# An attention layer's score products on four row strips of the array, and the next chunk's maxima moved into the present chunk's loop

## The chip, the cores and the metric

The kernel runs on one core of one Trainium2 chip. The metric is the device time of one execution in microseconds (us). Executions of one kernel agree within about 0.1% here. "Clock" is the TensorE clock that the profile records as granted, 1.00 being full speed. In the views, PE is TensorE, PEld the loading of its weights, DVE VectorE, ACT ScalarE and POOL GpSimd; L443 is line 443 of that kernel. PSUM is the memory to which the products are written; "a bank" stands below for the room of one tile of 512 columns in it.

## The reference

Four layers follow one another on x of shape (4, 64, 64, 128): a selective-scan block, an attention over all 4096 positions of an image, a convolution block and a neighborhood attention. Only layer 1, the attention, is touched. As the two kernels compute it, for each of the four images:

```
f = x @ Wq            # (4096, 16)
g = x @ Wk            # (4096, 16)
h = x @ Wv            # (4096, 128)
scores[n, m] = f[n] . g[m]
p = softmax over n of scores           # its maximum over n is subtracted first
x = x + gamma * (sum over n of h[n] * p[n, m])
```

The inner dimension of a score is 16. With one further row for the maximum to be subtracted it is 17, on an array of 128 rows.

## The kernel before

f and g lie transposed (channels on partitions). Row 32 of f is 1 and row 32 of g is minus the maximum, so that a product gives the shifted score. All other rows are zero, and every product spans all 128 rows. A first phase computes all scores only to take their maxima. A second computes them again, takes exp, and multiplies with the values; the scores of the next key tiles can be issued while exp runs, because four score tiles are in use.

```python
# phase 1: maxima
for j in range(NJ):                                    # 32 tiles of 128 queries
    for half in range(2):
        ps = psum.tile([128, 4, 512], F32, name="ps_max")          # two buffers
        for q in range(4):
            n0 = half * 2048 + q * 512
            nc.tensor.matmul(ps[:, q, :], gT[:, j * 128 : (j + 1) * 128], fT[:, n0 : n0 + 512], ...)
        nc.vector.tensor_reduce(mx[:, j, half : half + 1], ps, AX.XY, ALU.max)
# ... cut: minus the maxima go to row 32 of gT ...
# phase 2: exp and values
for c in range(NCH):                                   # 8 chunks of 512 queries
    # ... cut ...
    for j in range(NJ):                                # 32 tiles of 128 keys
        ps = psum.tile([128, 512], F32, name="ps_s", bufs=4)
        nc.tensor.matmul(ps, fT[:, j * 128 : (j + 1) * 128], gT[:, cols], start=True, stop=True)
        e = pool.tile([128, 512], F32, name="e", bufs=4)
        nc.scalar.activation(e, ps, AF.Exp)
        nc.tensor.matmul(pa, hv[:, j, :], e, start=(j == 0), stop=(j == NJ - 1))
        # ... cut: esum += e on VectorE ...
    # ... cut: denominator (ones x esum), reciprocal, product, x += gamma * ...
```

Of the kernel before, what the change touches and what calls it, by code (L numbers as in the profile page):

```python
"""Four layers on x (4, 64, 64, 128): a VMamba block (four-direction selective scan and an
MLP), an attention over all positions, a CSP conv block, a neighborhood-attention block.

Layouts, for one image of 4096 tokens and 128 channels:
- "rows":  [128, 32, 128], partition p and slot j hold token p * 32 + j  (layers 0 and 1)
- "tiles": [128, 32, 128], partition p and slot j hold token j * 128 + p (layer 3)
- transposed: channels on partitions, tokens along the free axis.
Layer 1 reshapes its (C, N) result to (N, C): row c, column j * 128 + p of it is token
c * 32 + j, channel p, which is the "rows" layout of its residual.
"""  # L10
# [28 lines left out]
# Neighborhood attention, by pairs of query rows: (first slot of the row's window among the  # L39
# eight key rows, first row of the position bias) for the upper and the lower query row.  # L40
# [3 lines left out]
def bc(ap, shape):  # L44
    return ap.to_broadcast(list(shape))


def mid(ap, n):
    """[p, f] -> [p, n, f], every n the same."""
    return bc(ap.unsqueeze(1), [ap.shape[0], n, ap.shape[1]])  # L50


# ---------------------------------------------------------------------------------------
# shared parts
# ---------------------------------------------------------------------------------------
# [19 lines left out]
def layernorm_T(tc, K, pool, psum, x, w, b, put):  # L75
    """LayerNorm over the channels of x [128, 32, 128]; put(g) is where the transposed,
    scaled and shifted slots 4g..4g+3 go, as [128 channels, 4, 128]."""
# [22 lines left out]
def mlp_residual(tc, K, pool, psum, x, xnT, w1, b1, w2, b2row):  # L100
    """x += gelu(xn @ w1 + b1) @ w2 + b2 for the 32 slots of x, xnT in the slots' order."""
# [19 lines left out]
def transpose_rows(tc, K, psum, x, xT):  # L121
    """x in "rows" -> xT [128 channels, 4096 tokens in order]."""
    nc = tc.nc
    view = xT.rearrange("c (p j) -> c j p", j=NJ)
    for g in range(NJ // 4):
        pt = psum.tile([128, 4, 128], F32, name="ps")
        for t in range(4):
            nc.tensor.transpose(pt[:, t, :], x[:, 4 * g + t, :], K.ident)
        if g % 2:
            nc.scalar.copy(view[:, 4 * g : 4 * g + 4, :], pt)  # L130
        else:
            nc.vector.tensor_copy(view[:, 4 * g : 4 * g + 4, :], pt)


# ---------------------------------------------------------------------------------------
# layer 0
# ---------------------------------------------------------------------------------------
# [38 lines left out]
def conv3x3(nc, out, lhsT, src, row0, nrows):  # L176
    """Accumulate the nine taps of a SAME 3x3 convolution into out [128, nrows, 64];
    src is [128, 64, 64], lhsT(tap) the weights. Taps off the image are left out."""
# [13 lines left out]
def layer0(tc, K, P, x):  # L192
    """x in "rows", updated in place."""
# [80 lines left out]
def selective_scan(tc, K, P, xc, yacc):  # L274
    """yacc = the four directions' scans of xc [128, 2, 4096], each with its skip term, on
    the tokens' own places. A direction runs over chunks of 512 tokens; the state after a
    chunk is the next one's initial value."""
    nc = tc.nc
    with ExitStack() as ctx:
# [3 lines left out]
        # The 40 rows (dt, B, C) of a chunk; the rest stays 0.  # L283
# [4 lines left out]
        def places(t, k, c):  # L288
            """Chunk c of direction k in t [128, 4096]: rows of the image, or columns."""
# [7 lines left out]
        def prepare(k, c, xdbl):  # L297
# [17 lines left out]
            # softplus(s) = max(s, 0) + log1p(e), e = exp(-|s|);  # L315
            # log1p(e) = ln(u) - ((u - 1) - e) with u = 1 + e as rounded.
# [57 lines left out]
# ---------------------------------------------------------------------------------------  # L374
# layer 1
# ---------------------------------------------------------------------------------------
def load_layer1(ctx, tc, K, A):
    nc = tc.nc
    pool = ctx.enter_context(tc.tile_pool(name="w1", bufs=1))
    P = SimpleNamespace()  # L380
    for name, shape in (("Wq", [128, 16]), ("Wk", [128, 16]), ("Wv", [128, C]), ("gamma", [128, 1])):
        t = pool.tile(shape, F32, name=f"w1_{name}")
        src = A[f"L1_conv_{name}"]
        nc.sync.dma_start(t, src.partition_broadcast(128) if name == "gamma" else src)
        setattr(P, name, t)
    return P


def layer1(tc, K, P, x):
    """x in "rows", updated in place. scores[n, m] = f[n] . g[m], softmax over n. Row 32 of  # L390
    f and g holds 1 and -max over n, so a product of the two is the shifted score. The other rows are 0,
    so that a product spans all 128 rows of the array."""
    nc = tc.nc
    with ExitStack() as ctx:
# [5 lines left out]
        mx = big.tile([128, NJ, 2], F32, name="mx")  # L400
        nmx = big.tile([128, NJ], F32, name="nmx")
        nc.gpsimd.memset(fT, 0.0)
        nc.gpsimd.memset(gT, 0.0)
        nc.gpsimd.memset(fT[32:33, :], 1.0)
        with tc.tile_pool(name="l1_ap", bufs=8, space=PSUM) as psum:
            transpose_rows(tc, K, psum, x, xT)
            for c in range(NCH):
                cols = slice(c * 512, (c + 1) * 512)
                for t, w in ((fT, P.Wq), (gT, P.Wk)):
                    ps = psum.tile([128, 512], F32, name="ps")  # L410
                    nc.tensor.matmul(ps[:16, :], w, xT[:, cols], start=True, stop=True)
                    nc.vector.tensor_copy(t[0:16, cols], ps[:16, :])  # L412
# [5 lines left out]
        with tc.tile_pool(name="l1_bp", bufs=2, space=PSUM) as psum:  # L418
            for j in range(NJ):
                for half in range(2):  # L420
                    ps = psum.tile([128, 4, 512], F32, name="ps_max")
                    for q in range(4):
                        n0 = half * 2048 + q * 512
                        nc.tensor.matmul(  # L424
                            ps[:, q, :], gT[:, j * 128 : (j + 1) * 128], fT[:, n0 : n0 + 512],
                            start=True, stop=True,
                        )
                    nc.vector.tensor_reduce(mx[:, j, half : half + 1], ps, AX.XY, ALU.max)  # L428
        nc.vector.tensor_reduce(nmx, mx, AX.X, ALU.max, negate=True)
        with tc.tile_pool(name="l1_c", bufs=3) as pool, tc.tile_pool(name="l1_cp", bufs=2, space=PSUM) as psum:  # L430
            for c in range(NCH):
                pr = psum.tile([1, 512], F32, name="pr", bufs=1)
                for t in range(4):
                    j = 4 * c + t
                    nc.tensor.transpose(pr[:, t * 128 : (t + 1) * 128], nmx[:, j : j + 1], K.ident)
                nc.vector.tensor_copy(gT[32:33, c * 512 : (c + 1) * 512], pr)
            for c in range(NCH):
                cols = slice(c * 512, (c + 1) * 512)
                pa = psum.tile([128, 512], F32, name="pa")
                esum = pool.tile([128, 512], F32, name="esum", bufs=2)  # L440
                for j in range(NJ):
                    ps = psum.tile([128, 512], F32, name="ps_s", bufs=4)
# [409 lines left out]
```

## Time and profile before

| | before |
|---|---|
| time, median | 17787.15 us (17784.28 to 17790.52, the 4 runs beside the changed kernel) |
| layer 1, first image, from the first f product to the last write of x | 717.6 us |
| of it maxima phase / exp and values | 224.9 / 468.7 us |
| granted clock, mean over the span | 0.961 |

"Layer 1 of an image" is counted in this way below, unless said otherwise; images 2 and 4 take some 17 us more in this kernel, because their f and g stage is interrupted (in image 2, VectorE waits 18.8 us for a GpSimd instruction on the weights of layer 2). The prediction counts from a little earlier (its 723.5 us), and so do the stretches of the first image below (694.8 us, which is 688.0 from the first f product).

The old loop in the timeline (start, length, engine, line, operation, out<-in; two records make one product of 512 columns):

```profile
3501.33 1.88 PE L443 MATMUL ps_s<-gT,fT 128*128 128x512 f32 x4
3503.05 1.98 PE L446 MATMUL pa<-e,hv 128*128 128x512 f32 x4
3504.86 1.88 PE L443 MATMUL ps_s<-gT,fT 128*128 128x512 f32 x4
3506.58 1.98 PE L446 MATMUL pa<-e,hv 128*128 128x512 f32 x4
```

Two score products, two value products, no gap: TensorE is the bound of this layer.

### The profile page before, as it was taken

Reading aid. Unit: us, or ns where it says so; the run is one execution under the profiler, and the core shown is the slowest. Engines: PE = TensorE matmul, PEld = TensorE weight load, DVE = VectorE, ACT = ScalarE, POOL = GpSimd, SP = SyncE. Lnnn points to the kernel's source line nnn. Section 1 sums busy time; section 2 is a strip of 40 time slices with the busy share of each in tenths; the row PEclk is TensorE's granted clock in tenths of the full one; section 3 lists DMA queues with packets and bytes.
Section 4 is the critical chain, followed back from the end, with each engine's and each line's share of the span. In section 5 each row is a group of like instructions: output and inputs, shape, how many; then the busy total and the mean of one; then the engine's idle time right before and its main releaser. Section 6 shows DMA issues by size and latency. Waiting matters only on the chain.

```text
span 17778.3 us, 113973 instructions
## 1 busy us (share of the span) xinstructions
PE 15481.1 (87%) x40816; PEld 6685.1 (38%) x40816; DVE 13330.6 (75%) x13760; ACT 5927.6 (33%) x10850; POOL 380.5 (2%) x667
## 2 busy tenths in 40 slices
PE   5888888998888879999998888889988888799999
PEld 2322223433223224356643223244332232344566
DVE  6999996539999994433359999965499999754333
ACT  1333333124333331322333333322243333313223
POOL 0000000000000001000000000000000000000000
PEclk9999999999999999999999999999999999999999
DMA  0000000000000000000000000000000000000000
GB/s 25 0 0 0 0 0 0 0 0 0 0 0 0 0 0 3 0 14 10 1 13 0 0 0 0 0 0 0 0 0 0 0 0 0 0 3 0 14 5 5
DMA packets 37609, 46.50 MB, mean 3 GB/s; under 512 B 14744, under 2 KB 32928, under 8 KB 34608
## 3 DMA queue, kind: packets, MB, share of 16 engines
q1 hardware_dynamic: 37040, 39.21, 0.7%
q8 instruction: 321, 5.26, 0.1%
q14 instruction: 248, 2.03, 0.0%
HBM read 25.57 MB, written 13.63 MB: 2 GB/s over the span
## 4 chain that ended last, share of the span: by engine, by line
DVE 42%; PE 38%; issue 18%; ACT 1%; POOL 1%; DMA 0%; SPq 0%; POOLq 0%; DVEq 0%; ACTq 0%
DVE h L355 28%; DVE dB L352 6%; PE pa L446 5%; PE ps_max L424 5%; PE ps_s L443 5%; PE ps L183 4%; DVE hC L361 3%; PE ps_s L722 3%; PE ps_s L723 3%; PE po L743 2%; PE ps L114 1%; PE pt L736 1%; PE ps L107 1%; DVE du L325 1%; DVE sp_ln L321 1%
## 5 line engine op out<-in xcount | busy, mean ns | idle before, releaser
L363 PE MATMUL py<-hC,ident 128*128 128x512 f32 x8192 | 4186.3, 635 | 506.3 <-DVE hC L361 497.2
L355 DVE TENSOR_TENSOR_SCAN h<-dA,state,dB 128x512 f32<-128x512 f32 x3584 | 4421.7, 1271 | 11.6 <-ACT dA L350 0.9
L347 PE MATMUL pb<-xdbl,ident 128*128 128x512 f32 x4096 | 2308.6, 651 | 1186.3 <-DVE dB L352 1180.5
L363 PEld LDWEIGHTS py<-hC,ident 128*128 128x128 f32 x8192 | 1474.0, 197 | 3327.6 <-DVE hC L361 1872.3
L350 ACT ACTIVATE dA<-delta,A 128x512 f32<-128x512 f32 x4096 | 2724.4, 712 | 1.5
L361 DVE TENSOR_TENSOR hC<-h,pc 128x1024 f32<-128x1024 f32 x2048 | 2486.7, 1214 | 0.4
L352 DVE TENSOR_TENSOR dB<-du,pb 128x1024 f32<-128x1024 f32 x2048 | 2454.7, 1199 | 0.4
L359 ACT COPY state<-h 128x2 f32<-128x2 f32 x2048 | 398.2, 194 | 6020.9 <-DVE h L355 6020.9
L347 PE MATMUL pc<-xdbl,ident 128*128 128x512 f32 x4096 | 2079.7, 594 | 0.1
L347 PEld LDWEIGHTS pb<-xdbl,ident 128*128 128x128 f32 x4096 | 684.6, 194 | 2609.8 <-DVE dB L352 2314.4
L450 DVE TENSOR_TENSOR esum<-esum,e 128x512 f32<-128x512 f32 x992 | 684.9, 690 | 964.9 <-ACT e L445 960.6
L347 PEld LDWEIGHTS pc<-xdbl,ident 128*128 128x128 f32 x4096 | 781.3, 191 | 992.8 <-issue 957.0
L445 ACT ACTIVATE e<-ps_s 128x512 f32<-128x512 f32 x1024 | 611.8, 598 | 1222.5 <-PE ps_s L443 1222.4
L446 PE MATMUL pa<-e,hv 128*128 128x512 f32 x2048 | 1017.0, 616 | 2.7 <-ACT e L445 2.7
L443 PE MATMUL ps_s<-gT,fT 128*128 128x512 f32 x2048 | 968.1, 594 | 0.0
L424 PE MATMUL ps_max<-fT,gT 128*128 128x512 f32 x2048 | 883.9, 594 | 33.3 <-DVE gT L412 31.8
L428 DVE TENSOR_REDUCE mx<-ps_max 128x1 f32<-128x2048 f32 x256 | 586.7, 2292 | 308.9 <-PE ps_max L424 308.9
L725 DVE TENSOR_REDUCE nmax<-ps_s 128x2 f32<-128x1024 f32 x256 | 313.5, 1225 | 476.9 <-PE ps_s L723 476.9
L729 ACT ACTIVATE e<-ps_s,nmax 128x512 f32<-128x512 f32 x512 | 347.6, 683 | 792.6 <-DVE nmax L725 792.6
L355 DVE TENSOR_TENSOR_SCAN h<-dA,dB 128x512 f32<-128x512 f32 x512 | 601.2, 1216 | 1.9 <-ACT dA L350 1.5
L424 PEld LDWEIGHTS ps_max<-fT,gT 128*128 128x128 f32 x2048 | 390.3, 191 | 524.3 <-issue 524.0
L443 PEld LDWEIGHTS ps_s<-gT,fT 128*128 128x128 f32 x2048 | 388.9, 191 | 481.3 <-issue 480.3
(213 smaller groups left out, 13307.3 us busy)
## 6 DMA issues: line engine op xcount, KB each, us to landing
bias<-bias_dram SPq DMA_DIRECT2D x10, 1024.0 KB, 9.1
x<-in_x SPq DMA_DIRECT2D x4, 2048.0 KB, 10.4
out<-x SPq DMA_DIRECT2D x4, 2048.0 KB, 8.7
bias_dram<-bt SPq DMA_DIRECT2D x5, 1024.0 KB, 3.9
w_fc_w<-in_L_conv_fc_w SPq DMA_DIRECT2D x8, 256.0 KB, 3.1
w_m_cv_w<-in_L_conv_m_cv_w SPq DMA_DIRECT2D x8, 144.0 KB, 3.1
w_in_proj_w<-in_L_conv_in_proj_w SPq DMA_DIRECT2D x2, 256.0 KB, 9.3
w_cv_bn<-in_L_conv_cv_bn SPq DMA_DIRECT2D x2, 256.0 KB, 3.4
```

Of the source, the lines that this page charges most:

```text
L183: nc.tensor.matmul(out[:, r0 - row0 : r1 - row0, c0:c1], lhsT((dy + 1) * 3 + dx + 1), src[:, r0 + dy : r1 + dy, c0 + dx : c1 + dx], start= ...
L347: nc.tensor.matmul(p, pick, xdbl, start=True, stop=True)
L350: nc.scalar.activation(dA[:, d, :], delta[:, d, :], AF.Exp, scale=P.A[:, k, d, n : n + 1])
L352: nc.vector.tensor_mul(dB, du, mid(pb, ND))
L355: nc.vector.tensor_tensor_scan(h[:, d, order], dA[:, d, order], dB[:, d, order], 0.0 if first else state[:, d, n : n + 1], ALU.mult, ALU.add,)
L361: nc.vector.tensor_mul(hC, h, mid(pc, ND))
L363: nc.tensor.matmul(py[:, d, :], K.ident, hC[:, d, :], start=(n == 0), stop=(n == NS - 1))
L424: nc.tensor.matmul(ps[:, q, :], gT[:, j * 128 : (j + 1) * 128], fT[:, n0 : n0 + 512], start=True, stop=True,)
L443: nc.tensor.matmul(ps, fT[:, j * 128 : (j + 1) * 128], gT[:, cols], start=True, stop=True)
L445: nc.scalar.activation(e, ps, AF.Exp)
L446: nc.tensor.matmul(pa, hv[:, j, :], e, start=(j == 0), stop=(j == NJ - 1))
L450: nc.vector.tensor_add(esum, esum, e)
```

## The change

The intent: f and g are written four times, on rows 0 to 16, 32 to 48, 64 to 80 and 96 to 112 (weights repeated along the columns, so at no extra product). Four score products, each on its own 17 rows, can then stand side by side in the array. And the phase of the maxima goes: while a chunk runs through exp and values, the maxima of the next one are computed in between, two tiles in each block of four key tiles. Half of the exp sums go to GpSimd.

```diff
+            def rows(i):
+                return slice(32 * i, 32 * i + 17)
+            def maxima(c):                      # a generator: 16 pairs for chunk c
...
+                    for q in range(4):
+                        ps = psum.tile([128, 2, 512], F32, name="ps_max")
+                        for u in range(2):
+                            r = rows(2 * (q % 2) + u)
+                            n0 = (2 * q + u) * 512
+                            nc.tensor.matmul(ps[:, u, :], gT[r, ...], fT[r, n0 : n0 + 512], ...)
+                        nc.vector.tensor_reduce(mx[:, t, q : q + 1], ps, AX.XY, ALU.max)
+                        if (t, q) != (3, 3):
+                            yield
...
+            for _ in maxima(0):                 # the first chunk's stand alone
+                pass
             for c in range(NCH):
+                ahead = maxima(c + 1) if c + 1 < NCH else iter(())
-                for j in range(NJ):
-                    ps = psum.tile([128, 512], F32, name="ps_s", bufs=4)
-                    nc.tensor.matmul(ps, fT[:, j * 128 : (j + 1) * 128], gT[:, cols], ...)
-                    nc.scalar.activation(e, ps, AF.Exp)
-                    nc.tensor.matmul(pa, hv[:, j, :], e, ...)
-                    ...
+                for b in range(NJ // G):        # G = 4
+                    ps = psum.tile([128, G, 512], F32, name="ps_s")        # one buffer
+                    for i in range(G):
+                        nc.tensor.matmul(ps[:, i, :], fT[rows(i), ...], gT[rows(i), cols], ...)
+                    e = pool.tile([128, G, 512], F32, name="e")
+                    nc.scalar.activation(e, ps, AF.Exp)
+                    for i in range(G):
+                        nc.tensor.matmul(pa, hv[:, j, :], e[:, i, :], ...)
+                    for eng, half in ((nc.vector, slice(0, 2)), (nc.gpsimd, slice(2, 4))):
+                        ...                     # esum += e, half on each engine
+                    for _ in range(2):
+                        next(ahead, None)
```

More of the change, by code (lines that the diff above doesn't have):

```diff
@@ L380, in load_layer1 @@
     P = SimpleNamespace()
-    for name, shape in (("Wq", [128, 16]), ("Wk", [128, 16]), ("Wv", [128, C]), ("gamma", [128, 1])):
+    for name, shape in (("Wq", [128, 128]), ("Wk", [128, 128]), ("Wv", [128, C]), ("gamma", [128, 1])):
         t = pool.tile(shape, F32, name=f"w1_{name}")
         src = A[f"L1_conv_{name}"]
-        nc.sync.dma_start(t, src.partition_broadcast(128) if name == "gamma" else src)
+        if name in ("Wq", "Wk"):
+            nc.gpsimd.memset(t, 0.0)
+            for i in range(4):
+                nc.sync.dma_start(t[:, 32 * i + 1 : 32 * i + 17], src)
+        else:
+            nc.sync.dma_start(t, src.partition_broadcast(128) if name == "gamma" else src)
         setattr(P, name, t)
+    P.first = pool.tile([128, 1], F32, name="w1_first")
+    nc.gpsimd.memset(P.first, 0.0)
+    for i in range(4):
+        nc.gpsimd.memset(P.first[32 * i : 32 * i + 1, :], 1.0)
     return P
@@ L393, in layer1 @@
     nc = tc.nc
+    G = 4
     with ExitStack() as ctx:
@@ L399, in layer1 @@
         hv = big.tile([128, NJ, C], F32, name="hv")
-        mx = big.tile([128, NJ, 2], F32, name="mx")
-        nmx = big.tile([128, NJ], F32, name="nmx")
-        nc.gpsimd.memset(fT, 0.0)
-        nc.gpsimd.memset(gT, 0.0)
-        nc.gpsimd.memset(fT[32:33, :], 1.0)
         with tc.tile_pool(name="l1_ap", bufs=8, space=PSUM) as psum:
@@ L408, in layer1 @@
                 cols = slice(c * 512, (c + 1) * 512)
-                for t, w in ((fT, P.Wq), (gT, P.Wk)):
-                    ps = psum.tile([128, 512], F32, name="ps")
-                    nc.tensor.matmul(ps[:16, :], w, xT[:, cols], start=True, stop=True)
-                    nc.vector.tensor_copy(t[0:16, cols], ps[:16, :])
+                ps = psum.tile([128, 512], F32, name="ps")
+                nc.tensor.matmul(ps, P.Wq, xT[:, cols], start=True, stop=True)
+                nc.scalar.activation(fT[:, cols], ps, AF.Identity, bias=P.first)
+                ps = psum.tile([128, 512], F32, name="ps")
+                nc.tensor.matmul(ps, P.Wk, xT[:, cols], start=True, stop=True)
+                nc.vector.tensor_copy(gT[:, cols], ps)
                 ph = psum.tile([128, 4, 128], F32, name="ps")
@@ L417, in layer1 @@
                 nc.scalar.copy(hv[:, 4 * c : 4 * c + 4, :], ph)
-        with tc.tile_pool(name="l1_bp", bufs=2, space=PSUM) as psum:
-            for j in range(NJ):
-                for half in range(2):
-                    ps = psum.tile([128, 4, 512], F32, name="ps_max")
-                    for q in range(4):
-                        n0 = half * 2048 + q * 512
-                        nc.tensor.matmul(
-                            ps[:, q, :], gT[:, j * 128 : (j + 1) * 128], fT[:, n0 : n0 + 512],
-                            start=True, stop=True,
-                        )
-                    nc.vector.tensor_reduce(mx[:, j, half : half + 1], ps, AX.XY, ALU.max)
@@ L429, in layer1 @@
-        nc.vector.tensor_reduce(nmx, mx, AX.X, ALU.max, negate=True)
-        with tc.tile_pool(name="l1_c", bufs=3) as pool, tc.tile_pool(name="l1_cp", bufs=2, space=PSUM) as psum:
-            for c in range(NCH):
-                pr = psum.tile([1, 512], F32, name="pr", bufs=1)
+        with tc.tile_pool(name="l1_c", bufs=2) as pool, tc.tile_pool(name="l1_cp", bufs=1, space=PSUM) as psum:
+            def rows(i):
+                return slice(32 * i, 32 * i + 17)
+            def maxima(c):
+                mx = pool.tile([128, 4, 4], F32, name="mx")
@@ L433, in layer1 @@
                 for t in range(4):
                     j = 4 * c + t
-                    nc.tensor.transpose(pr[:, t * 128 : (t + 1) * 128], nmx[:, j : j + 1], K.ident)
-                nc.vector.tensor_copy(gT[32:33, c * 512 : (c + 1) * 512], pr)
+                    for q in range(4):
[3 more added lines that the diff above has]
+                            n0 = (2 * q + u) * 512
+                            nc.tensor.matmul(
+                                ps[:, u, :], gT[r, j * 128 : (j + 1) * 128], fT[r, n0 : n0 + 512],
+                                start=True, stop=True,
+                            )
+                        nc.vector.tensor_reduce(mx[:, t, q : q + 1], ps, AX.XY, ALU.max)
+                        if (t, q) != (3, 3):
+                            yield
@@ new lines, in maxima @@
+                nmx = pool.tile([128, 4], F32, name="nmx")
+                nc.vector.tensor_reduce(nmx, mx, AX.X, ALU.max, negate=True)
+                pr = psum.tile([128, 512], F32, name="pr", tag="aux")
+                for t in range(4):
+                    nc.tensor.matmul(
+                        pr[:, t * 128 : (t + 1) * 128], bc(nmx[:, t : t + 1], [128, 128]), K.ident, start=True, stop=True
+                    )
+                g = gT[:, c * 512 : (c + 1) * 512]
+                nc.vector.scalar_tensor_tensor(g, pr, P.first, g, ALU.mult, ALU.add)
@@ L437, in layer1 @@
+                yield
+            for _ in maxima(0):
+                pass
             for c in range(NCH):
                 cols = slice(c * 512, (c + 1) * 512)
+                ahead = maxima(c + 1) if c + 1 < NCH else iter(())
                 pa = psum.tile([128, 512], F32, name="pa")
-                esum = pool.tile([128, 512], F32, name="esum", bufs=2)
-                for j in range(NJ):
-                    ps = psum.tile([128, 512], F32, name="ps_s", bufs=4)
-                    nc.tensor.matmul(ps, fT[:, j * 128 : (j + 1) * 128], gT[:, cols], start=True, stop=True)
-                    e = pool.tile([128, 512], F32, name="e", bufs=4)
-                    nc.scalar.activation(e, ps, AF.Exp)
-                    nc.tensor.matmul(pa, hv[:, j, :], e, start=(j == 0), stop=(j == NJ - 1))
-                    if j == 0:
-                        nc.vector.tensor_copy(esum, e)
-                    else:
-                        nc.vector.tensor_add(esum, esum, e)
@@ L451, in layer1 @@
-                pden = psum.tile([128, 512], F32, name="pden", bufs=1)
-                nc.tensor.matmul(pden, K.ones, esum, start=True, stop=True)
-                rec = pool.tile([128, 512], F32, name="rec", bufs=2)
+                esum = pool.tile([128, G, 512], F32, name="esum")
+                for b in range(NJ // G):
+                    ps = psum.tile([128, G, 512], F32, name="ps_s")
+                    for i in range(G):
+                        j = G * b + i
+                        nc.tensor.matmul(
+                            ps[:, i, :], fT[rows(i), j * 128 : (j + 1) * 128], gT[rows(i), cols], start=True, stop=True
+                        )
+                    e = pool.tile([128, G, 512], F32, name="e")
+                    nc.scalar.activation(e, ps, AF.Exp)
+                    for i in range(G):
+                        j = G * b + i
+                        nc.tensor.matmul(pa, hv[:, j, :], e[:, i, :], start=(j == 0), stop=(j == NJ - 1))
+                    for eng, half in ((nc.vector, slice(0, 2)), (nc.gpsimd, slice(2, 4))):
+                        if b == 0:
+                            eng.tensor_copy(esum[:, half, :], e[:, half, :])
+                        else:
+                            eng.tensor_add(esum[:, half, :], esum[:, half, :], e[:, half, :])
+                    for _ in range(2):
+                        next(ahead, None)
@@ L454, in layer1 @@
+                nc.vector.tensor_add(esum[:, 0:2, :], esum[:, 0:2, :], esum[:, 2:4, :])
+                pden = psum.tile([128, 512], F32, name="pden", tag="aux")
+                for i in range(2):
+                    nc.tensor.matmul(pden, K.ones, esum[:, i, :], start=(i == 0), stop=(i == 1))
+                rec = pool.tile([128, 512], F32, name="rec")
                 nc.vector.reciprocal(rec, pden)
-                att = pool.tile([128, 512], F32, name="att", bufs=2)
+                att = pool.tile([128, 512], F32, name="att")
```

## The prediction

> **What bounds the kernel now.** I read the page's cost groups first, then the busy time of each engine by stage of one image's layer 1, then the timeline inside a stage. Layer 1 (attention over all 4096 positions) runs four times, once per image. Its costliest groups on the page (busy us, mean ns of one; a 32-bit matmul of 512 columns is recorded as two MATMULs, so 1024 products are x2048):
>
> ```profile
> L446 PE MATMUL pa<-e,hv 128*128 128x512 f32 x2048 | 1017.0, 616 | 2.7 <-ACT e L445 2.7
> L443 PE MATMUL ps_s<-gT,fT 128*128 128x512 f32 x2048 | 968.1, 594 | 0.0
> L424 PE MATMUL ps_max<-fT,gT 128*128 128x512 f32 x2048 | 883.9, 594 | 33.3 <-DVE gT L412 31.8
> L428 DVE TENSOR_REDUCE mx<-ps_max 128x1 f32<-128x2048 f32 x256 | 586.7, 2292 | 308.9 <-PE ps_max L424 308.9
> L445 ACT ACTIVATE e<-ps_s 128x512 f32<-128x512 f32 x1024 | 611.8, 598 | 1222.5 <-PE ps_s L443 1222.4
> ```
>
> TensorE hardly waits; VectorE and ScalarE wait for it. The stages of the first image (columns: stretch, length, then busy us of PE, PEld, DVE, ACT, POOL, granted clock) are f/g/values, maxima, and exp with the products:
>
> ```profile
> 3105.50:3134.80 29.30, 27.05 (x128) 13.66 (x128) 14.92 (x21) 8.41 (x12) 4.01 (x2) 1.00 0.00 1
> 3134.80:3357.50 222.70, 219.97 (x512) 97.20 (x512) 146.88 (x65) 0.00 (x0) 0.00 (x0) 1.00 0.00 0
> 3357.50:3829.00 471.50, 464.49 (x1072) 179.50 (x1072) 216.51 (x291) 154.20 (x257) 0.00 (x0) 0.99 0.00 0
> ```
>
> So layer 1 is 723.5 us per image, 2894 us of 17778 (16%), and TensorE is busy 711.5 of each 723.5. Three sets of 256 products (maxima, scores, values) at 883.9/1024 = 0.863 us each make 663 of it. Nothing else in the program is changed: the built order differs only in layer 1 and its loads. The gain has to come out of the 2894 us.
>
> Two details of the old trace decide how the new form behaves. Layer 2 has the only matmuls that share the array now, two of 64 output columns:
>
> ```profile
> 7687.88 0.64 PE L568 MATMUL ps<-l_y,w_cv_w 128*64 128x512 f32 x1
> 7687.88 0.64 PE L569 MATMUL ps<-l_xT,w_cv2p_w 128*64 128x512 f32 x1
> ...
> 7688.36 0.59 PE L568 MATMUL ps<-l_y,w_cv_w 128*64 128x512 f32 x1
> 7688.36 0.59 PE L569 MATMUL ps<-l_xT,w_cv2p_w 128*64 128x512 f32 x1
> ```
>
> Both start together, and so do their second halves 0.48 us later: two 32-bit products side by side in the time of one, although one instruction's second half stands before the other's first half. And this is what a switch between the whole array and one row strip costs (L117 has one row of weights):
>
> ```profile
> 3101.60 0.48 PE L117 MATMUL ps<-w_fc_b,ones 1*128 1x128 f32 x2
> 3102.02 1.16 PE L114 MATMUL ps<-w_fc_w,mlp_h 128*128 128x128 f32 x8
> 3103.10 0.48 PE L117 MATMUL ps<-w_fc_b,ones 1*128 1x128 f32 x2
> ```
>
> Two L117 take 0.42 us start to start and eight L114 take 1.08; from 1.08 = 8s + w and 0.42 = 2s + w, s = 0.11 and the switch w = 0.2 us.
>
> [...]
>
> **The change part by part.** f and g stand four times, on rows 0-16, 32-48, 64-80, 96-112, at no extra matmul (128 weight columns instead of 16). This stage stays 29 us: the f copies move to ScalarE, which has room (8.4 busy).
>
> The 256-product maximum phase goes; only the first chunk's 16 pairs of products stay alone, with one two-bank buffer. One such pair: 0.86 us of matmuls side by side, 0.2 until the result is there (0.592 of one record minus 0.43 start to start, plus handoff), reduce of 1024 elements 1.23 (the row of layer 3's reduce of that size has 1225 ns), 0.05 handoff: 2.34 us. 16 x 2.34 + 2.5 for transposing the maxima = 40 us.
>
> The main loop, 64 blocks of four key tiles. From the built order on TensorE, between two value groups: one pair of maxima, four scores, one pair of maxima, four value products which wait for the exp of those same scores. The scores of the next block are not issued ahead of the value products, and one score buffer of four banks would forbid much of it. So the loop is a chain:
> - four value products, whole array: 4 x 0.86 = 3.43
> - switch to strips 0.2
> - a pair of maxima and four scores side by side: two layers of 0.86 plus a late first weight load 0.05 = 1.77
> - until the last score is written 0.2
> - exp over 2048 elements: 598 ns for 512 and 1044 for 1024 (the exp of layer 0) give 0.43 per further 512, so 1.88
> - handoff and the weights of the first value product 0.15
> Sum 7.63 us. The second maxima pair (it waits for the first pair's reduce: about 2.55 to 3.4 us after the value products end) fits before exp ends at 4.0. VectorE per block: two reduces 2.45, an add 1.21[...]. Two of these reduces and the GpSimd add lie beside the 3.43 of value products.
>
> Against it, the old loop took 4 x (2 x 0.86) plus small gaps, 3.53 us per two key tiles in the timeline, 7.06 per four, after a separate 222.7. So a block gets slower by about 0.6, and the whole maximum phase disappears into it.
>
> At a chunk's end the chain is longer: the last pair's reduce (1.23) can only follow GpSimd's last add, VectorE's add and the add of the two halves[...]; then maxima to rows 1.1 including a switch, rows into g 0.75, the denominator 1.9, the next scores 1.2, and the reciprocal (3.36, row L454's size) plus 0.68 must end before the next chunk's first value product may overwrite the one accumulator. Worked through, the next value product starts 15.5 us after exp against 7.6: +8, minus 0.5 for the pair that is missing in that block, 7.5.
>
> Per image: 29 + 40 + 56 x 7.63 (427) + 7 x 7.5 (52) + the last chunk without maxima 8 x 6.77 (54) + its end 8 = 610. Saved 113.5 per image, 454 in four, 2.6%: 17789 - 454 = 17335; I put down 17330.
>
> **The rivals.**
> - The strips do not run side by side. Then a pair plus four scores is 6 x 0.86 = 5.2 instead of 1.77, a block 11.0, and with the longer first chunk about 3.5 x 64 = 224 more per image: 17330 + 890 = 18200. Layer 2's pair speaks against it; for it speaks only that rows have never been packed here, and that each strip writes all 128 PSUM partitions.
> - They overlap only by half, because each product is two records and the second of one strip holds up the first of the next: six products staggered take 7 x 0.43 = 3.0, a block 8.9, +80 per image: about 17650, inside 2%. The pair in layer 2 started both first halves together, against this.
> - The chain through exp, not TensorE's work, is the new bound: TensorE would be free 1.2 us per block. I count this in already; it is why halving the score time doesn't give a third of the layer (the sum of pure TensorE work, 3.43 + 1.77 + 0.86, would allow 6.1 us a block and some 400 us more in all). If the exp wait were hidden the time would be 16940; the built order forbids that.
> [...]
> - The lone maximum phase runs TensorE at 37% busy, and the granted clock falls in sparse stages of layer 0 (0.77 in the variance stage, where one matmul record lasts 1061 ns instead of 592). Half clock there costs at most 14 us per image, 55 in all.
>
> **Range and chances.** A floor is a block of 7.3 and chunk ends of 4 take off another 84 + 98: 17150. Upward, partial overlap or slow GpSimd gives 17650. Between, 17433 is the 2% line; it is crossed when a block exceeds about 8.0 us. I hold full overlap at about 0.75 and the rest of the sum within 100 us, so faster 0.67, same 0.28, slower 0.05. Range 17190 to 17680.
>
> **What would show it.** Right: score matmuls of the four strips with starts a few ns apart, a block of 7.4 to 7.9 us, exp on 2048 elements at 1.88, TensorE's idle time before the value products put down to exp, at about 0.6 us per block, and layer 1 near 610 us per image. Wrong: strips starting 0.43 or 0.86 apart; a block set by GpSimd's adds or by VectorE's reduces; exp well over 1.9; a chunk end well over 8; any change outside layer 1.

## More of the kernel before

The clock's row in the page's 40 slices has no dip:

```profile
PEclk9999999999999999999999999999999999999999
```

## The result, and the profile after

The changed kernel takes 17650.64 us (17646.0 to 17653.1, 4 runs) against 17787.15 us, a ratio of 0.9923 with an interval of 0.9909 to 0.9937. The direction was right and the time lies inside the range, but the gain is 137 us where 457 were forecast. By the 2% line this counts as the same, for which the prediction had given a chance of 0.28. Most of the forecast gain is missing. That the time still lies inside the range (17190 to 17680) is luck: the upper end stood for half-overlapping strips or a slow GpSimd, and neither occurred.

The page's groups after the change (columns as in the prediction: busy us, mean ns of one, then the idle time before it and what ended it), and the page's row of the clock:

```profile
L482 PE MATMUL pa<-e,hv 128*128 128x512 f32 x2048 | 1148.2, 713 | 223.0 <-ACT e L479 163.0
L450 DVE TENSOR_REDUCE mx<-ps_max 128x1 f32<-128x1024 f32 x512 | 626.7, 1224 | 944.6 <-PE ps_max L446 944.6
L479 ACT ACTIVATE e<-ps_s 128x2048 f32<-128x2048 f32 x256 | 480.5, 1877 | 1886.2 <-PE ps_s L475 1886.2
...
PEclk9999999899999998899999999988999999989999
```

The value products are the same instructions on the same operands as before, yet their mean record has gone from 616 to 713 ns. The last line points to the reason: the clock's row now has dips, and only in slices that hold layer 1. The mean over the span fell from 0.961 to 0.938. The waits are about as forecast: the value products wait for exp, 163.0 us over 256 blocks, 0.64 us each, and the maxima go to 512 reduces of 1224 ns.

Layer 1 of the first image by stretches (columns: stretch, length, then busy us of PE, PEld, DVE, ACT, POOL, then the granted clock; the last two columns, DMA, play no part):

```profile
3100.40:3129.20 28.80, 26.13 (x140) 17.73 (x138) 9.94 (x13) 13.88 (x20) 0.00 (x0) 1.00 0.00 1
3129.20:3186.70 57.50, 36.22 (x78) 10.38 (x79) 20.51 (x18) 0.00 (x0) 0.00 (x0) 0.54 0.00 0
3186.70:3262.00 75.30, 66.10 (x199) 23.81 (x198) 38.84 (x26) 16.30 (x9) 18.97 (x8) 0.86 0.00 0
3262.00:3338.00 76.00, 65.74 (x208) 24.19 (x206) 44.16 (x30) 15.02 (x8) 18.40 (x8) 0.89 0.00 1
```

The stretches are: f, g and values; the first chunk's lone maxima; the first and the second chunk. The lone maxima run at 0.54, the chunks at 0.86 to 0.89. The old phases stood at 1.00 and 0.99.

Inside a chunk one sees two kinds of blocks. ScalarE's exp marks their length:

```profile
3286.42 1.88 ACT L479 ACTIVATE e<-ps_s 128x2048 f32<-128x2048 f32 x1 [5.77 <-PE ps_s L475]
3294.06 1.88 ACT L479 ACTIVATE e<-ps_s 128x2048 f32<-128x2048 f32 x1 [5.76 <-PE ps_s L475]
3303.40 1.88 ACT L479 ACTIVATE e<-ps_s 128x2048 f32<-128x2048 f32 x1 [7.46 <-PE ps_s L475]
3311.04 1.88 ACT L479 ACTIVATE e<-ps_s 128x2048 f32<-128x2048 f32 x1 [5.77 <-PE ps_s L475]
```

7.64 us, 9.34, 7.64. What is longer in the long block is TensorE's value group, the same eight records:

```profile
3295.99 5.40 PE L482 MATMUL pa<-e,hv 128*128 128x512 f32 x8 [0.43 <-ACT e L479]
...
3305.33 3.70 PE L482 MATMUL pa<-e,hv 128*128 128x512 f32 x8 [0.43 <-ACT e L479]
```

In the clock records of this trace the value is 1.0 or 0.5, nothing between; the shortest half-clock stretch lasts 3.41 us, and 182 of the 321 do. Around the long group above it is 1.00 from 3293.70 to 3297.13, where TensorE is busy for 2.53 of 3.43 us with products on 17 rows and the first value products, and 0.50 from 3297.13 to 3300.54. Most value records that lie in half clock last 1057 to 1061 ns instead of 592 (329 of 355). Of the 168 inner blocks of the four images, 109 have the short length, 58 the long one, and one lies between.

Where the missing time of an image is, forecast against the first image (us):

| part | forecast | measured | more |
|---|---|---|---|
| f, g, values | 29 | 28.8 | 0 |
| lone maxima of the first chunk | 40 | 57.5 | 17.5 |
| 42 inner blocks of chunks 1 to 7 | 320 (42 x 7.63) | 346.4 | 26 |
| six chunk ends, from the last block's exp to the exp of the next chunk's second block | 137 (6 x 22.8) | 166.1 | 29 |
| the rest (first block, seventh end, last chunk and its end) | 85 | 96 | 11 |
| sum | 611 | 694.8 | 84 |

Four times 84 us is 336, about the missing 320.

### The profile page after: what moved, and what is told of

It reads as the page before. It is cut to its first block, busy times and chain, and to the rows that moved or that the text cites. A ratio compares the mean times of both kernels' runs of the same rounds, so it can differ in the third digit from the quotient of the medians.

```text
span 17648.9 us, 112166 instructions
## 1 busy us (share of the span) xinstructions
PE 14931.2 (85%) x41008; PEld 6379.9 (36%) x41008; DVE 13244.9 (75%) x13276; ACT 5817.2 (33%) x10114; POOL 954.6 (5%) x925
## 4 chain that ended last, share of the span: by engine, by line
DVE 45%; PE 33%; issue 18%; ACT 3%; POOL 1%; DMA 0%; SPq 0%; ACTq 0%; POOLq 0%; DVEq 0%
DVE h L355 28%; DVE dB L352 6%; PE pa L482 6%; PE ps L183 4%; DVE hC L361 3%; PE ps_s L763 3%; PE ps_s L764 3%; PE po L784 3%; PE ps_max L446 2%; ACT e L479 2%; PE ps L114 1%; PE pt L777 1%; PE ps L107 1%; PE ps_s L475 1%; DVE du L325 1%
## 5 line engine op out<-in xcount | busy, mean ns | idle before, releaser
L355 DVE TENSOR_TENSOR_SCAN h<-dA,state,dB 128x512 f32<-128x512 f32 x3584 | 4433.3, 1277 | 10.8
L482 PE MATMUL pa<-e,hv 128*128 128x512 f32 x2048 | 1148.2, 713 | 223.0 <-ACT e L479 163.0
L450 DVE TENSOR_REDUCE mx<-ps_max 128x1 f32<-128x1024 f32 x512 | 626.7, 1224 | 944.6 <-PE ps_max L446 944.6
L479 ACT ACTIVATE e<-ps_s 128x2048 f32<-128x2048 f32 x256 | 480.5, 1877 | 1886.2 <-PE ps_s L475 1886.2
L446 PE MATMUL ps_max<-fT,gT 17*128 17x512 f32 x2048 | 693.3, 710 | 236.0 <-DVE mx L450 201.4
L482 PEld LDWEIGHTS pa<-e,hv 128*128 128x128 f32 x2048 | 440.3, 225 | 933.2 <-issue 554.4
L487 DVE TENSOR_TENSOR esum<-esum,e 128x1024 f32<-128x1024 f32 x224 | 531.2, 2372 | 171.2 <-ACT e L479 171.2
L487 POOL TENSOR_TENSOR esum<-esum,e 128x1024 f32<-128x1024 f32 x224 | 579.4, 2586 | 1340.8 <-ACT e L479 1340.8
L784 PEld LDWEIGHTS po<-v,eT 128*128 128x128 f32 x4096 | 506.4, 193 | 160.5 <-DVE eT L782 64.8
```

The source lines that it names most:

```text
L355: nc.vector.tensor_tensor_scan(h[:, d, order], dA[:, d, order], dB[:, d, order], 0.0 if first else state[:, d, n : n + 1], ALU.mult, ALU.add,)
L446: nc.tensor.matmul(ps[:, u, :], gT[r, j * 128 : (j + 1) * 128], fT[r, n0 : n0 + 512], start=True, stop=True,)
L482: nc.tensor.matmul(pa, hv[:, j, :], e[:, i, :], start=(j == 0), stop=(j == NJ - 1))
L487: eng.tensor_add(esum[:, half, :], esum[:, half, :], e[:, half, :])
L784: nc.tensor.matmul(po[:, hd, :], eT[:, q, :], v[:, vs[q], HD * hd : HD * hd + HD], start=(q == 0), stop=(q == 3),)
```

## The experiments

Two theories were on the table, and the letters are those used in what was expected. **A**: the granted clock follows the work in the array, and a product on few rows counts as little work. **B**: the clock follows TensorE's waiting (a busy array keeps its clock, whatever its rows), so that the new waits for exp and for the reduce brought it down. A further rival, **C**, was named for the second of the experiments on the old kernel: any product that uses only a part of the rows lowers the clock, however many rows it uses. Besides these, the runs had to show that the strips and the interleaving each do what the prediction's sum assumed.

### e1_rows32: strips on 32 rows

The strips span all 32 rows of their group instead of 17; the additional rows are zero in f and g, the instructions and the result are the same.

```diff
             def rows(i):
-                return slice(32 * i, 32 * i + 17)
+                return slice(32 * i, 32 * i + 32)
```

> The changed kernel with the strips' products over 32 rows (15 of them zero) instead of 17. Theory A (rows): [...]zero rows count as well, the loop's clock rises from 0.87 to at least 0.97, nearly all blocks (exp to exp) last 7.6 us instead of 7.6 and 9.3 in turn, layer 1 falls from 695 to about 640 us per image, the time to about 17440 us. The lone first maxima stay at half clock (57 us)[...]. Rival B (waiting): the clock falls because TensorE waits for exp and for reduces; the waits are unchanged, so clock 0.87, blocks of 7.6 and 9.3 and 17650 us stay.

Measured: 17595.93 us (17586.42 to 17606.36), ratio to before 0.9899 (0.9882 to 0.9915), clock 0.942. The rows alone, zeros at that, take off some 50 us: 55 against the changed kernel's 17650.64, which ran on another chip, or 46 when each is set against the kernel before on its own chip (183 and 137 us gained). B had no reason for that. But A's size was missed by 155 us. The blocks say why: 121 short and 47 long instead of 109 and 58. The rows move the clock, from 0.938 to 0.942 over the span; why it is by so little, the run does not show.

### e2_old_17_32: the old kernel's maxima on 17 and on 32 rows

In the kernel before, nothing is moved; the maxima products only read fewer rows, 17 for the first half of the tiles, 32 for the second. In that phase TensorE never waits. (Row 32 is not yet filled then, so the result stays correct.)

```diff
-                            ps[:, q, :], gT[:, j * 128 : (j + 1) * 128], fT[:, n0 : n0 + 512],
+                            ps[:, q, :], gT[: 17 if j < 16 else 32, j * 128 : (j + 1) * 128],
+                            fT[: 17 if j < 16 else 32, n0 : n0 + 512],
```

> The kernel before, its 256 maximum products over the first 17 rows for the first half of the tiles and over 32 for the second, one product at a time as before, so TensorE hardly waits there (about 98% busy). Theory A: [...]both halves run at half clock: record spacing 0.86 us instead of 0.43, the phase 440 instead of 223 us, the time about 18650 us. Rival B: no waiting, so full clock, 223 us and 17790 us.

Measured: 18645.86 us (one look), as A expected, clock 0.915. The first image's phase, the stretch with 17 rows and that with 32:

```profile
3134.80:3355.00 220.20, 220.20 (x259) 84.58 (x258) 73.33 (x32) 0.00 (x0) 0.00 (x0) 0.50 0.00 0
3355.00:3560.00 205.00, 205.00 (x242) 78.85 (x241) 68.74 (x30) 0.00 (x0) 0.00 (x0) 0.50 0.00 0
```

TensorE is busy for 220.20 of 220.20 us and for 205.00 of 205.00, and the granted clock is 0.50 in both. The whole phase took 440 to 443 us per image instead of 225 to 227. There is no waiting here to blame: theory B falls. On 128 rows the same products stand at 1.00 in the kernel before, on 17 and on 32 rows at 0.50.

### e2_old_64_96: the same on 64 and on 96 rows

```diff
-                            ps[:, q, :], gT[:, j * 128 : (j + 1) * 128], fT[:, n0 : n0 + 512],
+                            ps[:, q, :], gT[: 64 if j < 16 else 96, j * 128 : (j + 1) * 128],
+                            fT[: 64 if j < 16 else 96, n0 : n0 + 512],
```

> The same with 64 and 96 rows. Theory A: [...]full clock, 223 us for the phase and 17790 us. If instead any use of a part of the array lowers the clock (rival C), this runs at half clock like the one with 17 and 32 rows, about 18650 us.

Measured: 18112.38 us (one look), neither of the two numbers. The stretches are the first image with 64 and with 96 rows, then the second image with 64 and with 96 rows:

```profile
3136.10:3246.00 109.90, 109.82 (x256) 47.79 (x256) 71.05 (x31) 0.00 (x0) 0.00 (x0) 1.00 0.00 0
3248.00:3358.00 110.00, 108.34 (x253) 47.69 (x251) 73.25 (x33) 0.00 (x0) 0.00 (x0) 1.00 0.00 0
6839.00:7059.00 220.00, 217.43 (x255) 85.34 (x256) 73.45 (x36) 0.00 (x0) 0.00 (x0) 0.50 0.00 0
7065.00:7175.00 110.00, 108.65 (x251) 47.66 (x250) 72.31 (x32) 0.00 (x0) 0.00 (x0) 0.99 0.00 0
```

The same 64-row products take 110 us in one image and 220 in another. C falls by the first line: half of the rows kept the full clock, 1.00. In the second image the same products stood at 0.50, and the 96-row products after them at 0.99. Three phases longer by 108 to 111 us make up 328 of the 334 us between this run and the kernel before (17778.69 in these rounds). A expected 17790. That the clock at which a phase is entered makes the difference is the author's idea; no run tested it.

So these two runs give 0.50 with 17 and with 32 rows, 1.00 or 0.50 with 64, and 0.99 to 1.00 with 96. A rule for how many rows are enough, alone or beside waits, is not shown by them.

### e3_whole_array: the interleaving alone

The changed kernel with f and g once and every product on all 128 rows: same order, same waits, no strips.

```diff
-            for i in range(4):          # copies of the weights, and of the row of ones
+            for i in range(1):
...
             def rows(i):
-                return slice(32 * i, 32 * i + 17)
+                return slice(0, 128)
```

> The changed kernel with every score and maximum product over all 128 rows, so one after the other: the interleaving and larger tiles alone, without the strips. Theory A and the chain of the prediction: clock 1.0 in the loop, a block of 3.43 + 1.72 + 3.43 + 2.2 = about 10.8 us, layer 1 about 830 us per image, the time about 18200 us. If strips gave nothing on the path (the exp chain alone set the block), it would stay near 7.6 to 9.3 us a block and 17650 us. Rival B: waits of 0.5 to 2 us per block remain, so some windows still run at half clock.

Measured: 18141.24 us (one look), an inner block of 10.87 us, clock 0.960, about as A expected (18200 and 10.8).

```profile
L482 PE MATMUL pa<-e,hv 128*128 128x512 f32 x2048 | 980.8, 623 | 133.7 <-ACT e L479 133.7
L475 PE MATMUL ps_s<-gT,fT 128*128 128x512 f32 x2048 | 921.1, 592 | 0.0
```

Two things follow. The strips do run side by side in the changed kernel: they are worth 10.87 - 7.64 = 3.23 us a block at full clock, and the prediction's first rival had put the block without them at 11.0. And the waits alone don't cost the clock here: TensorE waits for exp in this run too (133.7 us, against 163.0 in the changed kernel), and the clock is 0.960 and the mean value record 623 ns, not 0.938 and 713. The interleaving without strips (with the exp over 2048 elements, the single score buffer and the sums on GpSimd that belong to it) makes the kernel 363 us slower than before.

### e6_filler: useless whole-array products in the thin places

On top of e1_rows32: one product of 256 columns, whole array, in each block but a chunk's first, and one of 512 columns after 12 of the 16 lone pairs. Their results are never read.

```diff
... between a pair of maxima products and its reduce:
+                        if c == 0 and q:
+                            junk = psum.tile([128, 512], F32, name="junk", tag="aux")
+                            nc.tensor.matmul(junk, K.ident, bc(mx[:, t, q - 1 : q], [128, 512]), ...)
... after a block's scores, reading the exp of the block before:
+                    if b:
+                        junk = psum.tile([128, 512], F32, name="junk", tag="aux")
+                        nc.tensor.matmul(junk[:, 0:256], K.ident, e[:, 3, 0:256], ...)
```

> The changed kernel with 32-row strips and, in the gaps where TensorE waits, one useless whole-array product whose result nobody reads: 512 columns after each lone first-chunk pair, 256 columns per block between the scores and the second maxima pair. It adds work and removes no wait of the chain. Theory A[...]: lone phase about 42 us instead of 57 with clock over 0.9, no blocks of 9.3 us, loop clock at least 0.96; the chunk ends keep some half-clock windows (28 down to about 27 us), so about 645 us per image and 17400 us in all. If the clock were not what lengthens the blocks, the extra product would leave blocks of 7.6 and 9.3 in turn or lengthen them by 0.2, and the time would be 17600 to 17750 us.

Measured: 17540.32 us (17534.94 to 17552.91), ratio 0.9864 (0.9849 to 0.9879), clock 0.945. In the inner blocks the filler did all that was asked of it: 168 of 168 have the short length, their sum is 321.0 us per image against 346 in the changed kernel, 341 with 32 rows, and the 320 of the prediction. TensorE does more here and is done sooner. The total missed its mark by 140 us because the other two places were not cured. At the chunk ends the one PSUM bank that the filler writes is also that of the maxima's rows and the denominator, and a chunk's first block got no filler; an end still takes 25.4 to 28.3 us. And the lone maxima (stretches of the first and of the second image):

```profile
3132.80:3181.70 48.90, 41.11 (x99) 12.33 (x100) 20.52 (x18) 0.00 (x0) 0.00 (x0) 0.83 0.00 0
...
6763.60:6830.30 66.70, 61.35 (x102) 16.82 (x103) 20.52 (x18) 0.00 (x0) 0.00 (x0) 0.50 0.00 0
```

In the first image the clock with the filler is 0.83 (0.54 in the changed kernel), and the stretch takes 48.9 us instead of 57.5. In the second it is 0.50 with the same filler. In the three others the filler is only a burden (64 to 67 us instead of 57.5 to 59.4). As in the 64-row run, the same products met different clocks in different images; why is not shown.

### e4_strips_old_order_32: the strips alone

The old two phases, with strips of 32 rows in both; exp by pieces of 512 as before, all sums on VectorE, four score tiles. (The four score products of a block are issued together, where the kernel before issued two at a time.)

```diff
-            def maxima(c): ...                                   # generator inside the loop
+            for j in range(NJ):
+                for half in range(2):
+                    ps = psum.tile([128, 4, 512], F32, name="ps_max")              # two buffers
+                    for q in range(4):
+                        nc.tensor.matmul(ps[:, q, :], gT[rows(q), ...], fT[rows(q), n0 : n0 + 512], ...)
+                    nc.vector.tensor_reduce(mx[:, j, half : half + 1], ps, AX.XY, ALU.max)
...
-                    ps = psum.tile([128, G, 512], F32, name="ps_s")
+                        ps = psum.tile([128, 512], F32, name="ps_s", bufs=4)       # for each i
...
-                    nc.scalar.activation(e, ps, AF.Exp)
+                        nc.scalar.activation(e, pss[i], AF.Exp)                    # for each i
...
-                    for _ in range(2):
-                        next(ahead, None)
```

> The strips alone (32 rows, four side by side) in the old order: a maximum phase of its own with two buffers of four banks, then exp in pieces of 512 with one key tile's value product each; no interleaving, no GpSimd. Expected: maximum phase set by VectorE's reduce of 2048 (2.29 + 0.05) x 64 = 150 us instead of 223; a block of four key tiles 0.2 + 0.96 + 0.2 + first exp 0.6 + 0.15 + 3.43 = 5.5 us instead of 7.06; layer 1 about 560 us per image, 17140 us in all, clock 1.0 in the loop. If instead the interleaving is what brings the gain, this is no faster than the changed kernel, 17650 us.

Measured: 17059.58 us (17059.07 to 17066.09), ratio 0.9593 (0.9579 to 0.9608). That is 80 us less than expected; layer 1 of the first image takes 537.9 us (some 7 more as the prediction counts) where about 560 were expected. The items that the expectation names make 29 + 150 + 64 x 5.5 = 531 of them. The maxima phase and the loop of the first image:

```profile
3131.20:3279.80 148.60, 100.92 (x537) 30.03 (x537) 143.62 (x67) 0.00 (x0) 0.00 (x0) 0.79 0.00 0
3279.80:3647.30 367.50, 320.54 (x1081) 120.37 (x1080) 214.13 (x287) 133.78 (x257) 0.00 (x0) 1.00 0.00 1
```

The first line has a bad clock, 0.79, and it costs nothing: VectorE is busy for 143.62 of 148.60 us and is the bound. The second line has a clock of 1.00; there the strips stand among whole-array value products, four to a block. So the strips in the old order gain 724 us, the interleaving without strips loses 363, and both together, with the same 32 rows (e1), gain 183: the interleaving takes away most of what the strips bring.

### e5_ahead_32 and e5_ahead_17: the next block's scores ahead of the wait

On top of e4: the four score products of the next block are issued before the present block's last value product, so that exp works beside the value products. Once with 32 rows, once with 17.

```diff
+            ready = scores(0, 0)
             for c in range(NCH):
                 for b in range(NJ // G):
+                    pss = ready
...
                     for i in range(G):
+                        if i == G - 1 and (c, b) != (NCH - 1, NJ // G - 1):
+                            nxt = (c, b + 1) if b + 1 < NJ // G else (c + 1, 0)
+                            ready = scores(*nxt)
                         nc.tensor.matmul(pa, hv[:, j, :], e, start=(j == 0), stop=(j == NJ - 1))
```

> The same with the next block's four scores issued before the last value product of the present block, so that exp lies beside value products. Expected: a block 3.43 + 0.96 + 2 switches of 0.2 + small = 4.85 us, layer 1 about 520 us per image, 16975 us in all. If TensorE's waits for exp were hidden already in the strips-alone form, the two would be equal, about 17140 us.

> The same over 17 rows instead of 32. Theory A: in the loop [...]whole-array products fill 3.43 of 4.85 us, so clock 1.0; in the maximum phase the clock is at half, but four products side by side then take 1.9 us against VectorE's 2.34, so nothing is lost: within 0.3% of the 32-row form, 16975 us. If narrow strips slowed the clock by themselves, the loop would fall to half clock in places, blocks over 5.5 us, 17200 us or more.

Measured: 16874.17 us (16872.12 to 16877.47), ratio 0.9488 (0.9474 to 0.9503), with 32 rows, and 16885.85 us (16883.07 to 16887.15), ratio 0.9495 (0.9479 to 0.9511), with 17. Both beat both kernels by far, 5.1% against before, and by 90 to 100 us more than expected: the loop came close (321 us for 64 blocks, 5.0 us each, 4.85 expected), but layer 1 took 491.2 us in the first image where 520 were expected, of which the items named make 29 + 150 + 64 x 4.85 = 489. The value products no longer wait, as the row of their idle time shows (32 rows):

```profile
L488 PE MATMUL pa<-e,hv 128*128 128x512 f32 x2048 | 951.9, 605 | 0.0
```

and the two phases of an image with 17 rows:

```profile
3130.00:3280.00 150.00, 134.63 (x531) 36.38 (x532) 144.87 (x67) 0.27 (x1) 0.00 (x0) 0.52 0.00 0
3281.00:3600.00 319.00, 316.51 (x1083) 120.59 (x1081) 212.83 (x284) 133.79 (x257) 0.00 (x0) 1.00 0.00 1
```

This closes the case from the other side. With 17 rows the maxima phase runs at 0.52, and takes 151.1 us instead of 148.5, because VectorE bounds it (busy for 144.87 of 150.00 us). The loop takes 321.0 us with 17 rows and 320.9 with 32, at a clock of 1.00 in both: there four score products on strips stand among four value products on the whole array in each block, and TensorE is busy for 316.51 of 319.00 us. In this kernel the 17 rows cost 12 us in all (16885.85 against 16874.17), and the half clock fell where TensorE was not the bound.

## Why the prediction was right or wrong

**Right: strips run side by side.** In a block of the changed kernel, four score records start at 3266.881, .888, .895 and .901 us, 7 ns apart, and their second halves 0.53 us later together. The prediction named starts a few ns apart; e3_whole_array gives the worth of it, 3.23 us a block. In the timeline these eight records take 1.14 us:

```profile
3266.88 1.14 PE L475 MATMUL ps_s<-gT,fT 17*128 17x512 f32 x8
```

**Right: the chain of a full-clock block.** 7.64 us measured, 7.63 worked out (the 0.05 to 0.2 us in it for handoffs and first weight loads were estimates); in the last chunk 6.82 and 6.77. exp over 2048 elements took 1877 ns (1.88). The reduce 1224 ns (1.23). And e6_filler's inner blocks sum to 321.0 us per image, against the forecast's 320.

**Right: GpSimd's add does not set the block.** The add of 1024 elements took 2.34 us (the median; up to 3.36), which no trace had shown before, as the old one has no plain add of that engine. VectorE's add of that size took 1.215 us at the shortest and 2.75 in the median of 224; why it is longer beside GpSimd's is not shown. VectorE's add and GpSimd's of the same block in the timeline:

```profile
3289.11 2.75 DVE L487 TENSOR_TENSOR esum<-esum,e 128x1024 f32<-128x1024 f32 x1
```

```profile
3288.44 2.34 POOL L487 TENSOR_TENSOR esum<-esum,e 128x1024 f32<-128x1024 f32 x1 [4.32 <-ACT e L479]
```

The VectorE one ends 1.08 us after GpSimd's. As forecast, this isn't the bound of a block: over the second chunk VectorE is busy for 44.16 of 76.00 us and GpSimd for 18.40.

**Right: nothing outside layer 1 matters.** Layer 1 became shorter by 29.6, 26.0, 32.9 and 32.8 us in the four images, 121 of the 129 us between the two profiled spans.

**Wrong: the clock.** The failing step stands in the last rival: "the granted clock falls in sparse stages of layer 0 … Half clock there costs at most 14 us per image, 55 in all." The prediction saw the low clock only where TensorE was idle much of the time, took idleness for its cause, and so looked for it only in the lone maxima, and there only as a rival. The chain of the loop, and that of the chunk end, were summed with full-clock durations throughout, although the prediction itself had TensorE free for 1.2 us of each 7.63. What the runs show: the maxima products on 17 or on 32 rows were granted 0.50 while TensorE was busy 100% of the time (e2_old_17_32), and the changed kernel's chunks, with six products on 17 rows and a wait of 0.64 us for exp in each block, 0.86 to 0.89, where the interleaving on 128 rows has 0.960 over its span (e3_whole_array; 0.938 in the changed kernel). That term of the sum was missing. By the table above it measures:

- Inner blocks: 26 us per image. Shown: with whole-array products added, it vanishes (e6_filler, 321.0 us instead of 346).
- Lone maxima: 17.5 us per image, in the place that the rival named. For the clock its 14 was about right: two pairs at full clock lie 2.46 to 2.51 us apart and the other 14 at half clock 3.40, which makes 13 us. The remaining 4.5 are two other terms: a full-clock pair takes 2.48 instead of 2.34 us, and the turn to the first chunk takes 4.9 instead of 2.5, where products of the next chunk's maxima come before the transposing, at half clock too.
- Chunk ends: 29 us per image. In part shown: 32 rows instead of 17 and nothing else took the six ends from 165.7 to 156.7 us per image (means of the four images, changed kernel and e1_rows32). No run cured the ends, so that the clock is all of it there is not shown.
- The remaining 11 us, in the first block, the seventh end and the last chunk, I have not taken apart; half-clock blocks are among them (10.8 and 8.3 us instead of 6.8 at the head of the last chunk).

The rest of what the chunk ends cost is read from the trace. At the first end of the first image:

```profile
3252.34 5.40 PE L482 MATMUL pa<-e,hv 128*128 128x512 f32 x8 [0.43 <-ACT e L479]
...
3263.57 3.38 PE L493 MATMUL pden<-esum,ones 128*128 128x512 f32 x4
...
3271.22 6.37 PE L482 MATMUL pa<-e,hv 128*128 128x512 f32 x8 [2.34 <-DVE att L497]
```

From the start of each to that of the next product, the last value group takes 5.33 us instead of the 3.63 of a short block, the denominator 3.31 instead of 1.72, and the next chunk's first value group 6.30 instead of 3.63, together 6.0 us more. The end of 28.4 less these 6.0 is 22.4, the forecast's 22.8.

Of the signs that the prediction named, a block of 7.4 to 7.9 us held for 109 of the 168 inner blocks, layer 1 near 610 us did not (694.8), and one sign of being wrong came true: a chunk end well over 8 us, 27.7 - 15.3 = 12.4 us beyond its two blocks on average in the first image.

**A rival not tested as it stood: the exp wait.** The prediction put the time without the wait at 16940 us and said that the built order forbids hiding it. e5_ahead_32 hides it, at 16874 us, but in another order, with the maxima in a phase of their own. So the run shows that the wait can be hidden and what that is worth there (185 us), and the nearness of the two numbers is no test. That the score buffer of four tiles in one piece, with two more banks for the maxima beside it, stood in the way is read from the kernel, not shown by a run.

## What to carry to other kernels

Packing small products into strips made them shorter here (3.23 us a block), but the clock fell where few rows were in use: 0.50 in the maxima on 17 or 32 rows, which had 1.00 on 128, and 0.86 to 0.89 in the changed kernel's chunks. So check the granted clock of every stage that gets strips, above all where a wait lies beside them; the busy time did not tell it (220.20 of 220.20 us at 0.50). Two ways out are measured here: whole-array products among the strips (e6_filler, where all 168 inner blocks came out short; e5_ahead_17, whose loop stood at 1.00), and strips in a stage that another engine bounds (e5_ahead_17's maxima, 151.1 us at 0.52, against 148.5 us at 0.78 with 32 rows). And try each half of a combined change alone: here the strips in the old order gave four times what they gave together with the interleaving, and hiding exp behind the value products gained a further 185 us, where removing a phase had cost time.
